# Third-stage scores from one 32-row product a batch, and the first stage without its fixed schedule of slots

## The chip, the cores and the metric

The kernel runs on one core of a Trainium2 chip. The time is the device time of one execution in microseconds, the median of three runs. The core has five engines that run side by side, each through its own list of instructions: TensorE (PE, with its weight loads as PEld), VectorE (DVE), ScalarE (ACT), GpSimd (POOL) and SyncE (SP), which here issues most DMAs. They wait for each other through semaphores.

## The reference, cut to what matters

The input x holds 128 batches of 128 tokens with 128 features, adj the edges of each batch. Four graph layers follow each other, each on a normalised and rectified copy of x and each added to x. Layer 0 averages neighbours by relation. Layer 1 builds weights from the differences of all pairs of tokens:

```
D = |x[:, :, None, :] - x[:, None, :, :]|
h = einsum('bijc,oc->bijo', D, W1) + b1       # 64 features a pair
m, v = mean and variance of h over all b, i, j
h = leaky((h - m) / sqrt(v + EPS) * g1 + be1)
s = where(A > 0, einsum('bijo,uo->biju', h, W2) + b2, NEG)
A = softmax(s, axis=-1)
```

The mean and variance run over all batches, so nothing of the second half of layer 1 can begin before all pairs have been multiplied. Layers 2 and 3 are attention layers with additive scores:

```
e_i = einsum('bnhd,d->bnh', h, a_i)           # one number a token and head
e_j = einsum('bnhd,d->bnh', h, a_j)
e = e_i[:, :, None, :] + e_j[:, None, :, :]
e = where(e > 0, e, 0.2 * e), then where(adj > 0, e, NEG)
attn = softmax(e, axis=2)
out = einsum('bijh,bjhd->bihd', attn, h)
```

Layer 2 has four heads of 32 features, layer 3 one head of 128.

## The kernel before, in words

The batches go in 32 groups of four (G = 4). The program has three stages.

**First stage: layer 0, and the pairs of layer 1.** Layer 0 of a group is a chain: load x, adj and agg; statistics and normalised copy hn; the mask of relation 1, its degree; transposes hT and maskT; products hw and po; normalisation with gamma and beta; the new x, its statistics and the normalised h1. Then h1 is transposed into xp (PSUM) and copied to xe (SBUF), with 64 columns repeated behind it, so that the feature column of token i + k is a shifted read. A batch has four tiles of pairs (NT = 4), each of 2 x 8 shifts. A tile takes four steps: the difference d = xe shifted - x (L399; tiles 0 and 2 on DVE, which reads x from xp, tiles 1 and 3 on POOL, which reads it from xe); its absolute value on ACT (L440); four products with W1 on PE into one of two hp buffers (L407); the evacuation hp to hs on ACT (L416), followed by the statistics of hs on DVE (L425, L426). Four tiles of hs fill one buffer of three, which SP stores to DRAM. d has two buffers for DVE and two for POOL.

All of this is written out by hand: slot(i) lists, for one tile number i, the difference of tile i + 2 (DVE) or i + 3 (POOL), the absolute value of tile i + 1, the products of tile i, the evacuation of tile i - 1 and the statistics of tile i - 2. features(g, half) puts the transposes and copies of two batches into given slots, with two buffers of xp, one for each half, and lets POOL copy the 64 repeated columns (L465). chain(g) puts each step of layer 0 into a slot from 22 slots ahead of the group; there hn is made on POOL (L508) and the last shift lnnb of h1 on POOL too (L195). manual_schedule keeps this order on every engine.

**Second stage: the rest of layer 1.** hs comes back from DRAM as z; the scores, the softmax and the output of layer 1 are formed. Its code is not touched.

**Third stage: layers 2 and 3.** group(g) is a generator; _staggered starts a new one every six steps, so that about five groups are under way. Here a scheduler places the instructions; so it also does for the code of the first stage that is not under manual_schedule. For each batch of layer 2, the scores e_i + e_j for four heads are summed in one PSUM tile pe by seven products: hT against A_i2, a weight column spread over 128 columns (L969), four products of A_j2 against hT (L971), a constant from the bias b_2 in three bf16 rows (L973), and the mask no_edge x off, which puts a large negative number where there is no edge (L974). Layer 3 does it with one product of 512 columns, four of 128 and the mask for the whole group (L1006, L1008, L1010). Then ACT copies pe to e (L900), DVE takes the maximum (L901) and the leaky rescale (L902), ACT the exponentials (L910), PE transposes e, ACT copies it to eT (L152), and PE multiplies with the values into pv (L989, L1021), which DVE divides by the sums (L991, L992, L1023). The normalisations take the root on POOL (L121, L122) between DVE's statistics (L127, L129) and its scaling h (L134).

Of the kernel before, what the change touches and what calls it, by code (L numbers as in the profile page):

```python
# [17 lines left out]
P = 128  # L18
G = 4
# [48 lines left out]
def tile_gnn_stack(ctx: ExitStack, tc: tile.TileContext, a: dict, out: bass.AP):  # L68
# [88 lines left out]

    with tc.tile_pool(name="c0", bufs=1) as c0, tc.tile_pool(name="p0", bufs=2) as p0:
# [12 lines left out]

        XP = [psum.tile([P, 3, P], F32, tag=f"xp{n}", name=f"xp{n}") for n in range(2)]
        gamma, beta = (t[:, 2, :] for t in XP)

# [33 lines left out]
        def layer0(g):  # L208
# [5 lines left out]
            agg = p0.tile([P, G, P], F32, name="agg")  # L214
            yield
# [35 lines left out]
            nc.vector.tensor_copy(o, po)  # L251
            yield "rest"
            nc.sync.dma_start(agg, AGG[g])
            nc.vector.tensor_tensor(o, o, agg, OP.add)
# [5 lines left out]
            for k in range(G):  # L260
                nc.vector.scalar_tensor_tensor(o[:, k, :], o[:, k, :], mv[:, k, 0:1], gamma,
                                               op0=OP.subtract, op1=OP.mult)
            yield
            on = sm("on")
            for k in range(G):
                nc.vector.scalar_tensor_tensor(on[:, k, :], o[:, k, :], rs[:, k:k + 1], beta,
                                               op0=OP.mult, op1=OP.add)
# [6 lines left out]
            H1[g] = p0.tile([P, G, P], F32, name="h1", bufs=3)  # L274
            act_norm(H1[g], x, RS1[:, g], nb)

# [5 lines left out]
        with tc.tile_pool(name="sc", bufs=1) as sc:  # L282
            top = highest(sc)
            flag = const.tile([1, 1], I32, name="flag")
            for t, v in ((gamma, "gamma"), (beta, "beta")):
                nc.vector.tensor_copy(t, load(v, [P, P], _bcast(a[v], P), pool=c0))
# [84 lines left out]

        jobs = {}

        def at(slot, engine, work):
            jobs.setdefault((slot, engine), []).append(work)  # L380

        def now(slot, engine):
            for work in jobs.pop((slot, engine), ()):
                work()

        XE, diffs, linear, halves, stats = {}, {}, {}, {}, {}

        def difference(i):

            b, t = divmod(i, NT)  # L390
            xe, k = XE[b // 2], b % 2
            on_pool = t in ON_POOL
            d = p0.tile([P, 2, KC, P], F32, tag=f"d{int(on_pool)}", name="d")
            x = xe[:, k, 0:P] if on_pool else XP[b // 2 % 2][:, k, :]
            ahead = xe[:, k, 1 + KC * t:]
            ahead = bass.AP(tensor=ahead.tensor, offset=ahead.offset,
                            ap=[list(ahead.ap[0]), [KH, 2], [1, KC], [1, P]])
            eng = nc.gpsimd if on_pool else nc.vector
            eng.tensor_tensor(d, ahead, x[:, None, None, :].to_broadcast([P, 2, KC, P]), OP.subtract)  # L399
            diffs[i] = d.rearrange("p h k i -> p h (k i)")  # L400

        def products(i):
            d = diffs.pop(i)
            hp = linear[i] = big("hp").rearrange("p a b -> p (a b)")
            for c in range(0, KC * P, 512):
                for hh in range(2):
                    nc.tensor.matmul(hp[64 * hh:64 * hh + 64, c:c + 512], w1T, d[:, hh, c:c + 512],  # L407
                                     start=True, stop=True)

        def evacuate(i):  # L410

            b, t = divmod(i, NT)
            if t == 0:
                halves[b] = p0.tile([P, NT, KC * P], F32, name="hs", bufs=3)
                stats[b] = small.tile([P, 9, 6], F32, name="st")
            nc.scalar.copy(halves[b][:, t, :], linear.pop(i))  # L416
            if t == NT - 1:
                nc.sync.dma_start(HP[b], halves[b])

        def statistics(i):  # L420

            b, t = divmod(i, NT)
            last = t == NT - 1
            hs, st = halves[b][:, t, :], stats[b]
            nc.vector.bn_stats(st[:, 2 * t, :], hs[:, 0:512])  # L425
            nc.vector.bn_stats(st[:, 2 * t + 1, :], hs[:, 512:1024 - P * last])  # L426
            if last:
                nc.vector.bn_stats(st[:, 8, :], hs[:, 1024 - P:])
                nc.vector.bn_aggr(ST1[:, b, 0, :], st.rearrange("p a b -> p (a b)"))
                nc.vector.bn_aggr(ST1[:, b, 1, :], st[:, 8, :])  # L430
                del halves[b], stats[b]

        def slot(i):
            n = NT * NB
            if 0 <= i + 2 < n and (i + 2) % NT not in ON_POOL:
                difference(i + 2)
            if 0 <= i + 3 < n and (i + 3) % NT in ON_POOL:
                difference(i + 3)
            if 0 <= i + 1 < n:
                nc.scalar.activation(diffs[i + 1], diffs[i + 1], AF.Abs)  # L440
            if 0 <= i < n:
                products(i)
            if 0 <= i - 1 < n:
                evacuate(i - 1)
            if 0 <= i - 2 < n:
                statistics(i - 2)
# [20 lines left out]
        def chain(g):  # L467
# [23 lines left out]
            def roots(last=False):  # L491
                rs = t["rs"] = RS1[:, g] if last else small.tile([P, G], F32, name="lnrs")
                rsqrt(rs, t["mv"][:, :, 1])
                if last:
                    t["nb"] = shift(t["mv"], rs)
# [570 lines left out]
```

## Time and profile before

| | |
|---|---|
| median of three runs | 3580.16 us (3574.61 to 3580.36) |
| the profiled execution's own time | 3580.16 us |
| its span | 3578.4 us |
| first stage, first to last absolute value | 89 to 1764 us |
| second stage, first to last score product | 1787 to 2757 us |
| third stage, first to last load's scaling and last output | 2809 to 3574 us |
| PE, DVE, ACT, POOL busy | 77%, 75%, 72%, 45% of the span |

Busy time is a union over the instructions of an engine. The duration of one instruction is longer than the distance to the next one's start where the two overlap; the distance between starts is what one costs in a dense row. A wait is put down to the instruction that ended it.

### The profile page before, as it was taken

To read this page: it belongs to the slowest core of one execution; us is meant where nothing else is said; L and a number is where in the kernel's file an instruction comes from. 1 tells how busy PE (TensorE), PEld (TensorE's weight loads), DVE (VectorE), ACT (ScalarE), POOL (GpSimd) and SP (SyncE) were. 2 spreads that over 40 slices of the span, in tenths; PEclk is the share of its full clock that TensorE was granted. 3 is DMA by queue.
4 is the path that set the end of the run, shared out by engine and by line. 5 is a ranking of instruction groups with operands and counts; after the bars stand their busy time and mean duration, and the time that the engine had idled before them with its cause. 6 is when DMAs were issued, how large, how long until landed. Compare 5 with 4: busy or idle time off the path is not lost.

```text
span 3578.4 us, 43595 instructions
## 1 busy us (share of the span) xinstructions
PE 2752.0 (77%) x15153; PEld 1351.2 (38%) x15153; DVE 2699.6 (75%) x5623; ACT 2593.5 (72%) x2987; POOL 1610.6 (45%) x1061
## 2 busy tenths in 40 slices
PE   1777776777777777777568888888887699999998
PEld 1222222222222222222123333333333577777776
DVE  4889888888888988988836666666666567777775
ACT  1988898898988989889756666666665366666664
POOL 2888888888889889888500000000000122222221
PEclk8989999999999999999879999999999799999998
DMA  6444444444444444444597888888885201111000
GB/s 220 162 176 183 171 177 188 182 173 174 188 176 168 185 188 176 179 174 176 205 365 266 326 325 326 325 326 326 326 326 193 79 30 36 36 34 33 22 25 18
DMA packets 168626, 659.10 MB, mean 184 GB/s; under 512 B 31312, under 2 KB 83408, under 8 KB 118224
## 3 DMA queue, kind: packets, MB, share of 16 engines
q1 hardware_dynamic: 165264, 643.65, 47.3%
q0 software_dynamic: 2560, 8.39, 0.8%
q10 hardware_dynamic: 576, 4.19, 0.3%
q8 instruction: 123, 2.02, 0.2%
q14 instruction: 103, 0.84, 0.1%
HBM read 340.76 MB, written 315.42 MB: 183 GB/s over the span
## 4 chain that ended last, share of the span: by engine, by line
PE 32%; DVE 26%; POOL 16%; ACT 11%; issue 10%; DMA 3%; SPq 0%; POOLq 0%; ACTq 0%; DVEq 0%
POOL d L399 10%; PE ps L691 8%; ACT d L440 5%; DVE z L696 4%; PE pt L151 3%; PE pk L713 3%; PE pv L989 3%; DVE d L399 3%; ACT hs L416 3%; DMA z<-hp 3%; PE hp L407 2%; DVE st L425 2%; DVE st L426 2%; PE pr L928 2%; ACT e L910 2%
## 5 line engine op out<-in xcount | busy, mean ns | idle before, releaser
L407 PE MATMUL hp<-d,w1T 128*64 128x512 f32 x4096 | 1059.6, 640 | 426.0 <-ACT hs L416 298.4
L399 POOL TENSOR_TENSOR d<-xe 128x2048 f32<-128x2048 f32 x256 | 1074.6, 4198 | 51.0 <-PE hp L407 48.4
L440 ACT ACTIVATE d<-d 128x2048 f32<-128x2048 f32 x512 | 988.8, 1931 | 57.9 <-POOL d L399 55.2
L407 PEld LDWEIGHTS hp<-d,w1T 128*64 128x64 f32 x4096 | 281.6, 142 | 1102.7 <-issue 721.8
L399 DVE TENSOR_TENSOR d<-xe,xp 128x2048 f32<-128x2048 f32 x256 | 580.1, 2266 | 11.3 <-POOL xe L465 7.7
L416 ACT COPY hs<-hp 128x1024 f32<-128x1024 f32 x512 | 523.1, 1022 | 1.2 <-PE hp L407 1.2
L425 DVE BATCH_NORM_STATS2 st<-hs 128x6 f32<-128x512 f32 x512 | 351.5, 687 | 197.5 <-ACT hs L416 196.2
L121 POOL TENSOR_SCALAR scale<-mv 128x1 f32<-128x1 f32 x1 | 0.2, 222 | 1020.7 <-DVE mv L827 1020.7
L691 PE MATMUL ps<-z,w2z 128*32 128x512 f32 x1024 | 225.1, 711 | 178.3 <-DVE z L696 164.8
L426 DVE BATCH_NORM_STATS2 st<-hs 128x6 f32<-128x512 f32 (+1 forms) x512 | 329.2, 643 | 0.0
L696 DVE SCALAR_TENSOR_TENSOR z<-z 128x2048 f32<-128x2048 f32 x128 | 291.7, 2279 | 2.5 <-ACT z L695 2.5
L700 ACT ACTIVATE zr<-z,bias,scale 128x2048 f32<-128x2048 f32 x128 | 266.7, 2084 | 30.8 <-issue 15.0
L900 ACT COPY e<-pe 128x512 f32<-128x512 f32 x160 | 93.7, 586 | 264.3 <-PE pe L974 262.3
L695 ACT ACTIVATE z<-z,bias,scale 128x2048 f32<-128x2048 f32 x128 | 266.6, 2082 | 15.9 <-DMA z<-hp 15.5
L121 POOL TENSOR_SCALAR lnrs<-lnmv 128x4 f32<-128x4 f32 x128 | 30.9, 241 | 546.2 <-DVE lnmv L129 484.8
L691 PE MATMUL ps<-z,w2l 128*32 128x512 f32 x1024 | 268.7, 688 | 0.0
L691 PE MATMUL ps<-zr,w2r 128*32 128x512 f32 x1024 | 241.1, 631 | 0.6 <-ACT zr L700 0.6
L910 ACT ACTIVATE e<-e,mx 128x128 f32<-128x128 f32 x640 | 209.3, 390 | 14.2 <-DVE mx L907 12.5
L713 PEld LDWEIGHTS pk<-pick,su 128*128 128x128 f32 x1024 | 124.3, 192 | 114.8 <-ACT y L783 24.1
L151 PE MATMUL pt<-ident,e 128*128 128x128 f32 x768 | 128.1, 294 | 40.2 <-DVE e L763 29.9
L971 PEld LDWEIGHTS pe<-hT,spread 128*128 128x128 f32 x1024 | 133.4, 193 | 47.0 <-issue 47.0
L713 PE MATMUL pk<-pick,su 128*128 128x16 f32 x1024 | 136.2, 265 | 6.8 <-DVE su L707 6.5
(226 smaller groups left out, 4468.2 us busy)
## 6 DMA issues: line engine op xcount, KB each, us to landing
hp<-hs SPq DMA_DIRECT2D x128, 2048.0 KB, 6.3
z<-hp SPq DMA_DIRECT2D x256, 1024.0 KB, 13.1
x<-x SPq DMA_DIRECT2D x128, 256.0 KB, 5.8
u<-rows SPq DMA_DIRECT2D x32, 384.0 KB, 11.5
x<-in_x_dram SPq DMA_DIRECT2D x32, 256.0 KB, 7.7
adj<-in_adj_dram SPq DMA_DIRECT2D x32, 256.0 KB, 8.1
agg<-a SPq DMA_DIRECT2D x32, 256.0 KB, 7.6
z<-y SPq DMA_DIRECT2D x32, 256.0 KB, 7.2
```

What stands on the lines that cost most here:

```text
L399: eng.tensor_tensor(d, ahead, x[:, None, None, :].to_broadcast([P, 2, KC, P]), OP.subtract)
L407: nc.tensor.matmul(hp[64 * hh:64 * hh + 64, c:c + 512], w1T, d[:, hh, c:c + 512], start=True, stop=True)
L416: nc.scalar.copy(halves[b][:, t, :], linear.pop(i))
L425: nc.vector.bn_stats(st[:, 2 * t, :], hs[:, 0:512])
L426: nc.vector.bn_stats(st[:, 2 * t + 1, :], hs[:, 512:1024 - P * last])
L440: nc.scalar.activation(diffs[i + 1], diffs[i + 1], AF.Abs)
L691: nc.tensor.matmul(ps[32 * c:32 * c + 32, :], w[:, w0:w0 + 32], v[:, 512 * c:512 * c + 512], start=j0 == 0, stop=j0 > 0 and i == 1, skip_g ...
L695: nc.scalar.activation(z0, z0, AF.Identity, bias=bias1, scale=scale1[:, 0:1])
L696: nc.vector.scalar_tensor_tensor(z0, z0, 0.01, z0, op0=OP.mult, op1=OP.max)
L700: nc.scalar.activation(zr, z1, AF.Relu, bias=bias1, scale=scale1[:, 0:1])
L713: nc.tensor.matmul(pk[:, kk, 0:16], su[:, kk, :], pick.rearrange("p h j -> p (h j)"), start=True, stop=True)
L910: nc.scalar.activation(e[:, q, :], e[:, q, :], AF.Exp, bias=mx[:, t, q:q + 1], accum_out=None if sums is None else sums[:, t, q:q + 1])
```

## The change

It has two parts.

In the first stage, the slots, features and chain are gone. Layer 0 of every group is the generator layer0, which existed before for the first two groups, woven with a generator pairs(g) by _weave, three steps of layer0 for four of pairs. The scheduler orders the instructions. There is one xp for the four batches of a group in place of two for two batches each; xe has two buffers of four batches in place of three of two; ACT makes both parts of xe; hn is made on ACT; gamma and beta lie in a PSUM tile of their own.

In the third stage, e_i and e_j are computed by token: hT of each batch is the weight, and eight columns (layer 3: two) are the moving operand. DVE writes the result into a tile of tokens whose other columns are one, with 32 columns a batch, and PE transposes it: after that, each batch owns 32 rows, in which e_i stands beside ones and ones beside e_j. ACT copies the left side, DVE multiplies the right side with a constant pattern that keeps one head (layer 3: one batch) a block of columns. One fp32 product of 32 rows (layer 3: of all 128) then gives e_i + e_j for all heads, and the mask follows as before. The bias is added in the tokens. A new group starts every seven steps.

```diff
+    def pairwise(pool, xe, xp, k, t):
+        on_pool = t in ON_POOL
+        d = pool.tile([P, 2, KC, P], F32, tag=f"d{int(on_pool)}", bufs=2, name="d")
+        x = (xe if on_pool else xp)[:, k, 0:P]
...
+        eng = nc.gpsimd if on_pool else nc.vector
+        eng.tensor_tensor(d, ahead, x[:, None, None, :].to_broadcast([P, 2, KC, P]), OP.subtract)
+        d = d.rearrange("p h k i -> p h (k i)")
+        nc.scalar.activation(d, d, AF.Abs)
+        hp = big("hp").rearrange("p a b -> p (a b)")
+        for c in range(0, KC * P, 512):
+            for hh in range(2):
+                nc.tensor.matmul(hp[64 * hh:64 * hh + 64, c:c + 512], w1T, d[:, hh, c:c + 512],
+                                 start=True, stop=True)
+        return hp
+
+    def pair_stats(pool, xe, xp, k, b):
+        st = small.tile([P, 9, 6], F32, name="st")
+        hs = pool.tile([P, NT, KC * P], F32, name="hs", bufs=3)
+        for t in range(NT):
+            yield
+            hp = pairwise(pool, xe, xp, k, t)
+            nc.scalar.copy(hs[:, t, :], hp)
+            nc.vector.bn_stats(st[:, 2 * t, :], hs[:, t, 0:512])
...
-        XP = [psum.tile([P, 3, P], F32, tag=f"xp{n}", name=f"xp{n}") for n in range(2)]
-        gamma, beta = (t[:, 2, :] for t in XP)
+        affine = psum.tile([P, 2, P], F32, tag="affine", name="affine")
...
+        def pairs(g):
+            h = H1.pop(g)
+            xp = psum.tile([P, G, P], F32, tag="xp", name="xp")
+            for k in range(G):
+                nc.tensor.transpose(xp[:, k, :], h[:, k, :], ident)
+            xe = p0.tile([P, G, P + 2 * KH], F32, name="xe")
+            nc.scalar.copy(xe[:, :, 0:P], xp)
+            nc.scalar.copy(xe[:, :, P:], xp[:, :, 0:2 * KH])
+            for k in range(G):
+                yield from pair_stats(p0, xe, xp, k, g * G + k)
...
-        with tc.manual_schedule():
-            for g in range(NG):
-                for half in range(2):
-                    features(g, half)
-                if g >= AHEAD:
-                    chain(g)
-            for i in range(-5, NT * NB + 2):
-                slot(i)
+        for g in range(NG):
+            _weave(pairs(g), layer0(g + AHEAD) if g + AHEAD < NG else iter(()), 0.75)
...
+        def sides(g, hT, wa, n):
+            ps = sm("ps")
+            for k in range(G):
+                nc.tensor.matmul(ps[:, k, 0:2 * n], hT[:, k, :], wa, start=True, stop=True)
+            t = tokens[n][g % 3]
...
+            if n == 4:
+                nc.vector.tensor_tensor(to, ps_k, add_b.rearrange("p (s h) -> p s h", s=2)[:, None, :, :]
+                                        .to_broadcast([P, G, 2, n]), OP.add)
+            else:
+                nc.vector.tensor_copy(to, ps_k)
+            yield
+            pt = sm("pts", "pt")
+            for side in range(2):
+                nc.tensor.transpose(pt[:, side, :], t[:, side, :, :].rearrange("p k c -> p (k c)"), ident)
+            yield pt
...
+            got = []
+            yield from last_of(sides(g, hT, wa2, 4), got)
+            left = p2.tile([P, P], F32, name="left")
+            nc.scalar.copy(left, got[0][:, 0, :])
+            right = p2.tile([P, 4, P], F32, name="right")
+            nc.vector.tensor_tensor(right, got[0][:, 1:2, :].to_broadcast([P, 4, P]),
+                                    heads[:, :, None].to_broadcast([P, 4, P]), OP.mult)
...
-                    nc.tensor.matmul(pe, hT[:, k, :], A_i2, start=True, stop=False, skip_group_check=True)
-                    for hd in range(4):
-                        nc.tensor.matmul(pe[:, hd, :], A_j2[:, hd, :], hT[:, k, :], start=False,
-                                         stop=False, skip_group_check=True)
-                    nc.tensor.matmul(pe, ones3, b_parts, start=False, stop=False, skip_group_check=True)
+                    rows = slice(32 * k, 32 * k + 32)
+                    nc.tensor.matmul(pe, left[rows, :], right[rows, :, :], start=True, stop=False,
+                                     skip_group_check=True)
...
-            nc.tensor.matmul(pe, A_j3[:, 0, :], hT, start=True, stop=False, skip_group_check=True)
-            for k in range(G):
-                nc.tensor.matmul(pe[:, k, :], hT[:, k, :], A_i3[:, 0, :], start=False, stop=False,
-                                 skip_group_check=True)
+            nc.tensor.matmul(pe, left, right, start=True, stop=False, skip_group_check=True)
...
-        _staggered((group(g) for g in range(NG)), 6)
+        _staggered((group(g) for g in range(NG)), 7)
```

## The prediction

> **What bounds the kernel now.** I read the busy time by stage first, then the waits of the engine that is fullest in each stage the change touches, then the timeline of one period. The span is 3578.4 us; the profiled execution's own time is 3580.16 us, which is also the median shown, so 1.8 us lie around the span and no correction is needed.
>
> By stage (busy us and instructions of each engine, granted clock, DMA):
>
> ```profile
> core 0: us, PE busy (x) PEld busy (x) DVE busy (x) ACT busy (x) POOL busy (x), PEclk, DMA share, GB/s
> 200.00:1400.00 1200.00, 870.32 (x3720) 302.64 (x3720) 1051.56 (x1993) 1073.63 (x929) 1025.34 (x587) 0.94 0.45 178
> 1770.00:2800.00 1030.00, 800.33 (x5064) 342.45 (x5064) 658.67 (x1088) 607.67 (x417) 1.56 (x4) 0.88 0.82 305
> 2892.00:3486.00 594.00, 576.58 (x3937) 465.50 (x3937) 423.82 (x1346) 370.01 (x1009) 129.63 (x181) 1.00 0.11 32
> ```
>
> First stage: ACT 89%, DVE 88%, POOL 85%: three nearly full engines. Third stage: PE 97%, DVE 71%, ACT 62%. The second stage's instruction order is the same in both programs on every engine, so I leave it alone.
>
> Who keeps ACT idle in those 1200 us (total, times, longest), and what lies there on POOL and ACT:
>
> ```profile
> ACT h L555 <- POOL lnnb L195: 67.3, 23, 3.1
> ACT d L440 <- POOL d L399: 39.6, 45, 1.5
> ACT xe L461 <- PE xp L457: 14.0, 14, 1.7
> ACT maskT L521 <- PE pt L518: 5.3, 12, 0.5
> ```
>
> ```profile
> 1020.07 0.23 POOL L121 TENSOR_SCALAR RS<-MV 128x4 f32<-128x4 f32 x1 [4.94 <-DVE MV L489]
> 1021.79 0.25 POOL L195 TENSOR_SCALAR lnnb<-lnnb 128x4 f32<-128x4 f32 x1
> 1022.00 4.18 POOL L399 TENSOR_TENSOR d<-xe 128x2048 f32<-128x2048 f32 x1
> 1075.36 0.25 POOL L195 TENSOR_SCALAR lnnb<-lnnb 128x4 f32<-128x4 f32 x1
> ```
>
> The four waits sum to 126.2 us, all of ACT's idle time (1200 - 1073.6). L195 runs once a group of four batches; eight of its steps, from 704.15 to 1127.60, give 52.93 us a group (the two shown are one of them). So ACT works 47.4 us and waits 5.6 us a group of 16 tiles. Between starts, an absolute value L440 costs 1.81 us, an evacuation L416 0.89.
>
> Third stage, PE, one batch, and the same instruction one group later; then the waits there:
>
> ```profile
> 3200.31 1.02 PE L969 MATMUL pe<-spread,hT 128*128 128x512 f32 x2
> 3201.17 1.05 PE L971 MATMUL pe<-hT,spread 128*128 128x128 f32 x8
> 3202.15 0.38 PE L973 MATMUL pe<-b_parts,ones 3*128 3x512 bf16 x1
> 3202.47 0.39 PE L974 MATMUL pe<-off,no_edge 128*128 128x512 bf16 x1
> 3202.70 1.02 PE L969 MATMUL pe<-spread,hT 128*128 128x512 f32 x2
> 3223.09 1.02 PE L969 MATMUL pe<-spread,hT 128*128 128x512 f32 x2
> ```
>
> ```profile
> DVE sums L991 <- PE pv L989: 97.1, 52, 7.8
> DVE h L134 <- POOL lnrs L122: 45.1, 52, 0.9
> PE pv L1021 <- ACT eT L152: 17.4, 26, 0.7
> ```
>
> A batch of scores costs 2.39 us between starts (0.86 + 0.98 + 0.32 + 0.23), a group 22.78 us, of which PE idles about 0.7. DVE waits for PE in long pieces; its wait for POOL's root is 0.86 us, twice a group.
>
> [...] DVE stands 0.86 us before an h at 3202.67, waiting for POOL's root, though the rescale L902 queued behind it has had its maximum since 3201.82 (L901 from 3201.13, 0.69 long). So the built order of each engine, which carries no times, decides with the durations here. [...] No 32-row product is in this trace; in the second stage, eight records of L713 between 32-column products take 0.99 us, against 0.86 for eight of the sixteen of L989 (1.71)[...].
>
> **First stage, worked out.** Added on ACT: the normalisation hn moves there from POOL, 4 x 0.395 = 1.58 us (a pair of h takes 0.79). xe is copied once a group in two pieces (0.50 + 0.27) for two copies of 0.30: +0.17. ACT's work becomes 47.4 + 1.75 = 49.1 us. POOL loses hn (3.15) and two copies (0.29 each), gains a shift (0.45): it is not the bound. DVE gains a small maximum.
>
> The waits follow from the new order at each group's start. ACT runs: xe in two pieces, evacuation 15 of the old group, abs of tile 1 (POOL's), abs of tile 0, the four h, abs of tile 3 (POOL's), abs of tile 2, evacuation 0. There is one xp buffer, so xe can't be made before tile 14's difference is done. Clock from the end of xe:
> - Evacuation 15 needs its product: 0.45 to 1.34.
> - POOL's difference of tile 1 takes 4.2: abs 1 at 4.3 to 6.1, abs 0 to 7.9. ACT idles 3.0.
> - POOL runs tile 3's difference next (to 8.6), then root 1.12 and shift 0.54: lnnb at 10.3. The four h wait until then: 2.4 idle; they end at 11.9.
> - abs 3 to 13.7, abs 2 to 15.5, evacuation 0 to 16.4; then ACT is dense but for 0.3 before evacuation 4, whose product queues behind four transposes.
> - Tile 14's difference ends at 47.8 on DVE, xp's transposes and product 14 at 52.7, evacuation 14 at 54.1, the next xe at 55.
>
> 49.1 + 0.45 + 3.0 + 2.4 + 0.3 = 55.2; the walk gives 55.0. I take 55.1, 2.2 us over 52.93. For 30 groups 66 us; the last two, without layer 0 beside them, pay the same start, some 3 us each: **+72 us**. The head (h at 82 us, behind the DMA of agg) keeps its releaser. If the new dense stretch has slack I overlooked, the period falls to about 54.4 (+50); if tile 14's difference slips past product 13, which has 0.4 us of slack, about 56 (+95).
>
> **Third stage, worked out.** Removed on PE a group: 4 x 2.39 for layer 2, and 0.86 + 0.90 + 0.22 for layer 3 (L1006, L1008, L1010): 11.5 us. Added: 4 x (0.90 + 0.23); two side products of four 128-row weights with 8 and 2 columns, by L989's 0.107 a record 8 x 0.107 = 0.86 each; four transposes 0.44; layer 3's 1.1: 7.8. PE's work falls from about 22 to 18.2 us. DVE gains two 128x512 products from PSUM (0.60 each, by L1023) and two small writes (0.14, by L717): from 423.8/594 x 22.78 = 16.3 to 17.7. ACT gains two copies of 128x128, about 0.2 each.
>
> No engine is full then, so I followed the order around one period. It has two halves in series. DVE half, from the reciprocal that waits for pv of one group to the h whose transposes PE needs next: reciprocal, max, o, rescale, three statistics, aggregates, right, small: 3.2; wait for POOL's root 0.87; h and small 1.1; two maxima and two rescales 2.4; statistics, aggregates 1.07; reciprocal, two maxima, small 1.5; two rescales 1.2; h 1.03: 12.4 us. PE stands in the transposes of h meanwhile. PE half, from there to the pv that the reciprocal awaits: hand-over and last transpose 0.17; e 0.44; pv 0.86; sides 0.86; pr 0.95; e and sides 1.3; po 0.93; sides' transposes 0.22; pv 0.86; e 0.44; wait 0.56 for layer 3's right, which DVE can make only after po and that pv; scores 1.13; pv 1.71; tail 0.13: 10.6. Sum 22.9 against 22.78: PE's 3.7 us turn into waits for DVE. 31 steps of 0.15 are +5 us, and the longer path at fill and drain +3: **+8 us**.
>
> Unknown costs. The 32-row products [...] stand where PE waits anyway, beside the DVE half; I take nothing. A side product could cost its weight loads' own 0.19 a record, +0.7 each: +45 us in all; or less than a 33-column one, 0.3 each, -19. right could cost 0.1 more: +6. Set-up: six fills on POOL behind the weights' DMA, against a spread of 1.68 us and the three-part split that go: between -3 and +3; I take nothing.
>
> Forecast: 3580.16 + 72 + 8 = **3660 us**.
>
> **Rivals.**
> - Third stage bound by its busiest engine (ends faster): if the two halves overlap and PE stays as full as now, the period is 18.2/0.97 = 18.8 us, 31 x 4.0 = -123: 3580 + 72 - 123 = 3529. It decides below 20.5 us, where 72/31 us a group pay for the first stage. For it: PE's 97% now. Against: DVE's 17.7 plus two root waits of 0.86 already make 19.4, and its reciprocal sits behind pv.
> - First stage unchanged: POOL, with 41 us of work in 53, gets ahead and the new waits vanish: 3588. Against: POOL can't start before xe exists.
> - Both worse: a missed product makes the first stage 57 us a group (+123 to +125), side products cost their loads: 3580 + 125 + 50 = 3755. For it: slack of 0.4 us.
> - The scores' part does nothing because PE was not the bound: excluded by 97%; it does what it says, and DVE is late next.
>
> **How the numbers follow.** My forecast 0.72, third stage faster 0.09, first stage unchanged 0.06, both worse 0.13. Its own bounds, +50 to +95 and -15 to +55, not all at one end, give 3605 to 3720; for the rivals I widen to 3598 to 3728. A measurement of this kernel tells about 0.2% from no change. Faster than that: 0.09; within it: 0.03, half of the first-stage rival; slower: 0.88.
>
> **What would show it.** First stage: about 55 us a group; ACT's longest waits before abs of POOL's tile and before h, at group starts. Third stage: still about 23 us a group, PE near 80%, PE waiting for DVE's h, DVE waiting for PE's pv and po. I am wrong if the third stage's period is under 21, or the first stage's is 53.

## The result, and the profile after

The changed kernel takes 3825.35 us (3821.53 to 3828.12, four runs), the kernel before beside it 3577.68 us: a ratio of 1.0692, with a 95% interval of 1.0673 to 1.071. It is 247.7 us slower; the prediction was 80 us slower, and its range ended at 3728 us.

From the trace, the first product of the second stage starts at 1945.6 us instead of 1787.0: +158.6 us for the first stage. The second stage has its old length. The rest, some 88 us, is the third stage.

The table by stage of the changed kernel (columns as in the prediction's first table: busy us and instructions of each engine, granted clock, DMA):

```profile
core 0: us, PE busy (x) PEld busy (x) DVE busy (x) ACT busy (x) POOL busy (x), PEclk, DMA share, GB/s
200.00:1400.00 1200.00, 850.21 (x3412) 276.11 (x3408) 986.80 (x1846) 1029.94 (x941) 875.44 (x440) 0.86 0.40 164
1930.00:2960.00 1030.00, 800.96 (x5064) 342.71 (x5064) 658.38 (x1091) 607.21 (x416) 2.02 (x6) 0.88 0.81 305
3073.00:3720.00 647.00, 626.90 (x3310) 434.30 (x3309) 462.15 (x1452) 395.93 (x1066) 130.57 (x182) 0.80 0.10 29
```

The column to look at is the one after POOL. The granted clock of TensorE (the share of its full rate that it was given) fell from 0.94 to 0.86 in the first stage and from 1.00 to 0.80 in the third; the untouched second stage keeps 0.88. In the third stage PE is again busy 97% of the time, although the change took work from it: the same products last longer (1.12 us becomes 2.07 for one of four in the timeline below).

The first stage in the timeline, PE's products L175 (start, us, and in brackets the idle time before and who ended it). Eight records are one tile, sixteen are two:

```profile
1015.93 1.94 PE L175 MATMUL hp<-d,w1T 128*64 128x512 f32 x8 [0.77 <-ACT d L171]
1025.59 6.38 PE L175 MATMUL hp<-d,w1T 128*64 128x512 f32 x16 [7.72 <-ACT d L171]
1033.98 5.35 PE L175 MATMUL hp<-d,w1T 128*64 128x512 f32 x16 [2.01 <-ACT hs L187]
1039.85 1.94 PE L175 MATMUL hp<-d,w1T 128*64 128x512 f32 x8
1044.70 3.63 PE L175 MATMUL hp<-d,w1T 128*64 128x512 f32 x8 [2.33 <-ACT d L171]
```

A tile takes 1.94 us, but after PE has stood still for 7.7 us at a group's start, two take 6.38; two more take 5.35 behind a wait of 2.0, and one takes 3.63 behind a wait of 2.3. The clock is 0.5 for 10.2 us from 1020.9, and for 3.4 us each from 1034.5 and 1044.8: 17 us of a 58-us group. The kernel before has such places too, but fewer: 6.1 us of a 53-us group on average (138 us of half clock between 200 and 1400 us). One of them:

```profile
1025.70 5.37 PE L407 MATMUL hp<-d,w1T 128*64 128x512 f32 x16 [2.37 <-ACT hs L416]
1032.56 1.94 PE L407 MATMUL hp<-d,w1T 128*64 128x512 f32 x8 [1.49 <-ACT hs L416]
```

What ScalarE waits for in the 1200 us of the table's first row (total, times, longest):

```profile
ACT d L171 <- POOL d L169: 60.9, 21, 2.9
ACT hs L187 <- PE hp L175: 58.4, 89, 1.4
ACT h L239 <- POOL lnnb L233: 47.1, 21, 2.2
```

The first and third rows are the waits that the prediction placed at a group's start (2.9 and 2.25 us, where 3.0 and 2.4 were expected). The middle row was not in its sum: 58.4 us in 21 groups, 2.8 us a group.

The third stage, PE's score products of one group:

```profile
3402.39 1.12 PE L848 MATMUL pe<-right,left 32*128 32x512 f32 x2
3403.44 0.39 PE L850 MATMUL pe<-off,no_edge 128*128 128x512 bf16 x1
3403.76 1.12 PE L848 MATMUL pe<-right,left 32*128 32x512 f32 x2
3404.81 0.39 PE L850 MATMUL pe<-off,no_edge 128*128 128x512 bf16 x1
3405.43 1.12 PE L848 MATMUL pe<-right,left 32*128 32x512 f32 x2 [0.23 <-DVE right L839]
3406.48 0.39 PE L850 MATMUL pe<-off,no_edge 128*128 128x512 bf16 x1
3406.80 2.07 PE L848 MATMUL pe<-right,left 32*128 32x512 f32 x2
```

The fourth takes nearly double the others, without a gap before it to speak of (0.23 us in the five before). The clock stays at 0.5 from 3407 to 3414. Outputs leave 23.3 to 26.5 us apart, 24.92 us on average over the first 27 groups, against 22.8 for most groups before. The stage's filling, before its first output, ran at a clock of 0.60, where the kernel before had 0.80, and took some 22 us more than before.

### The profile page after: what moved, and what is told of

It reads as the page before. It is cut to its first block, busy times and chain, and to the rows that moved or that the text cites. A ratio compares the mean times of both kernels' runs of the same rounds, so it can differ in the third digit from the quotient of the medians.

```text
span 3825.5 us, 42248 instructions
## 1 busy us (share of the span) xinstructions
PE 2917.1 (76%) x14385; PEld 1329.6 (35%) x14385; DVE 2767.7 (72%) x5773; ACT 2682.0 (70%) x3171; POOL 1508.8 (39%) x913
## 4 chain that ended last, share of the span: by engine, by line
PE 41%; ACT 21%; DVE 18%; issue 8%; POOL 6%; DMA 4%; SPq 0%; POOLq 0%; DVEq 0%; ACTq 0%
ACT d L171 11%; PE hp L175 8%; PE ps L531 7%; ACT hs L187 7%; PE pe L848 5%; PE pt L151 4%; POOL d L169 4%; DVE z L536 4%; DMA z<-hp 3%; PE pv L865 3%; PE pk L553 3%; DVE d L169 2%; DVE st L188 2%; DVE st L190 2%; PE pr L798 1%
## 5 line engine op out<-in xcount | busy, mean ns | idle before, releaser
L175 PE MATMUL hp<-d,w1T 128*64 128x512 f32 x4096 | 1147.5, 694 | 502.8 <-ACT d L171 437.6
L175 PEld LDWEIGHTS hp<-d,w1T 128*64 128x64 f32 x4096 | 291.5, 155 | 1189.8 <-ACT d L171 636.3
L848 PE MATMUL pe<-right,left 32*128 32x512 f32 x256 | 213.7, 926 | 2.4 <-DVE right L839 2.4
L151 PE MATMUL pt<-ident,e 128*128 128x128 f32 x768 | 157.9, 330 | 46.9 <-DVE e L603 29.8
L151 PEld LDWEIGHTS pt<-ident,e 128*128 128x128 f32 x768 | 113.8, 175 | 112.6 <-issue 84.5
```

Of the source, the lines that this page charges most:

```text
L151: nc.tensor.transpose(pt[:, k, :], src[:, k, :], ident)
L848: nc.tensor.matmul(pe, left[rows, :], right[rows, :, :], start=True, stop=False, skip_group_check=True)
```

## Experiments

Two questions. Are the half-clock stretches a cause of the time, or do they only mark waits that would be there anyway? And what brings them on: gaps on PE, or the new kinds of product? Differences in the table are against the kernel before, run beside each. An edit can shift the order in which the scheduler puts the instructions; where two kernels are compared, the text says whether they share it.

| run | what it is | us | against before |
|---|---|---|---|
| e1_third | third-stage change alone | 3671.67 | +98.2 |
| e2_first | first-stage change alone | 3731.31 | +157.8 |
| e4_fill4, e5_fill6, e6_fill12 | whole change, 4, 6, 12 fillers a group | 3817.74, 3815.75, 3820.21 | +244.3, +242.4, +246.9 |
| e8_fill_both | 12 + 8 fillers | 3751.59 | +178.2 |
| e3_rows128 | e1, masked product of 128 rows | 3677.28 | +103.8 |
| e7_all128 | e1, products of 128 rows | 3650.89 | +77.5 |
| e9_wide32 | e1, token products 64 wide | 3623.07 | +49.7 |
| e10_wide128 | both | 3611.04 | +37.7 |
| e14_gap6 | e1, six steps | 3874.72 | +301.1 |
| e16_wide6_rows32 | e14, 64 wide | 3775.09 | +198.0 |
| e11_gap6 | e10, six steps | 3555.96 | -17.4 |
| e12_masked6, e13_wide6, e15_masked5 | six or five steps, split by batch kept | 3590.06, 3604.13, 3681.25 | +16.4, +30.5, +107.6 |
| e17_pool6, e18_diag | the same | 3658.31, 3626.17 | +81.2, +52.4 |

### The two halves apart

The first run has the first stage of before and the third stage of the change; the second is the reverse.

> The change to the third stage alone; the first stage keeps its fixed schedule of slots. If the two halves of the change add up as the trace of the changed kernel divides them, this gives the kernel before plus about 88 us, near 3666 us, with a period of about 24.1 us a group in the third stage. If half of that loss was carried in from the first stage (a clock that is granted less because of what ran earlier), less than 40 us is left.

> The change to the first stage alone; the third stage keeps its old scores. If the halves add up, the kernel before plus about 159 us, near 3737 us, with a period of about 58 us a group. If the first stage's loss depends on what the third stage prepares (tables, pools), it differs from 159 by more than 20 us.

Measured: +98.2 us (ratio 1.0267, 1.0241 to 1.0293) and +157.8 us (1.0444, 1.0424 to 1.0464), together 256 against 248 for the whole. The halves add up, each has its own loss, and the third stage's is there with a first stage that runs as before: its clock is 0.80 from 2950 to 3550 us in the first of the two runs, 0.98 in the second. So the two are studied apart.

### First stage: fill PE's gaps

Filler products give PE more to do and nothing else. If they make the kernel faster all the same, the clock is the likely reason.

```diff
-        affine = psum.tile([P, 2, P], F32, tag="affine", name="affine")
+        affine = psum.tile([P, 4, P], F32, tag="affine", name="affine")
...
+            for n in range(4):
+                nc.tensor.matmul(affine[:, 2:4, :], ident, xe[:, 0:2, 0:P], start=True, stop=True)
```

> The changed kernel with four filler products (128x256, fp32[...]) a group in the first stage, issued right after the copy of xe, in TensorE's longest gap of 7.7 us; the order of ScalarE, VectorE and GpSimd is not changed. Theory A (that gap lowers the clock of the products after it, which ScalarE then waits for): the gap is cut to about 5.5 us, the two products after it take under 5 us in place of 6.4, and the first stage's period falls from 58.0 by 1 to 3 us, so 30 to 85 us off the kernel although TensorE does more. Theory B (ScalarE's waits come from the order alone): no change within 10 us.

> The changed kernel with six filler products (128x256, fp32) a group after the copy of xe in the first stage; one exponent of the order of ScalarE shifts by a tile against the changed kernel, so this run is only the partner of the one with twelve, whose instructions stand in the same order on every engine apart from the fillers. Six fillers take about 2.9 us, so about 5 us of TensorE's longest gap is left. Both theories: near 3815 us.

> The same order with twelve fillers, about 5.9 us, so that under 2 us of the longest gap is left. Theory A (the gap lowers the clock of the products behind it and ScalarE waits for these): the clock there stays at 1.0, the first two tiles behind the gap take about 4 us in place of 6, and the kernel is 30 to 80 us faster than with six fillers. Theory B (the waits come from the order alone): the same time within 10 us, or slower.

Four fillers shortened the gap only to 5.8 us; the clock fell all the same, and the time, +244.3 us, is the changed kernel's +247.7 within what the runs scatter. Six and twelve fillers, in one order, gave 3815.75 and 3820.21 us: theory B seems to win. The twelve did what they should at their place:

```profile
1019.86 5.45 PE L329 MATMUL affine<-xe,ident 128*128 128x256 f32 x24
1027.67 3.65 PE L175 MATMUL hp<-d,w1T 128*64 128x512 f32 x16 [2.37 <-ACT d L171]
1036.99 8.38 PE L175 MATMUL hp<-d,w1T 128*64 128x512 f32 x24 [5.66 <-ACT d L171]
```

The two tiles behind the filled gap took 3.65 us in place of 6.38. But a second gap, 5.66 us, follows, and the three tiles behind it took 8.38 us, where 3 x 1.94 would be 5.8. The loss had moved: ScalarE's waits of this kind were 72.3 us in 21 groups, not fewer. The period stayed at 58.0 us for most groups of all three runs, which also fits a cycle that has nothing to do with the clock. So the second gap was filled too, with eight more behind the second tile of each group, and no other engine's order changed in the steady groups:

```diff
+        for n in range(8 if (k, t) == (0, 1) else 0):
+            nc.tensor.matmul(fills[0], ident, xe[:, 0:2, 0:P], start=True, stop=True)
         return hp
```

> As the run with twelve fillers a group, and eight more after the second tile of each group, in the second long gap of TensorE (5.7 us); ScalarE, VectorE and GpSimd keep that run's order in the steady groups. Theory A (half-clock products behind gaps cause ScalarE's waits): no half-clock stretch is left in the first stage, ScalarE no longer waits 1.6 and 1.2 us for products, the period falls from 58.0 to about 55 us and the kernel is 60 to 90 us faster than with twelve fillers. Theory B (another cycle holds the period at 58.0 us): the period stays at 58.0 us whatever the clock.

Measured: 3751.59 us, 68.6 us less than with twelve fillers, although PE does eight products a group more. The table of its first stage:

```profile
200.00:1400.00 1200.00, 992.43 (x4420) 435.72 (x4422) 1047.74 (x1925) 1064.41 (x976) 907.14 (x456) 0.97 0.42 171
```

The clock is 0.97 (one stretch of 3.4 us a group is left), ScalarE's waits of 1.6 and 1.2 us for products are gone, and xe is copied every 55.0 us, with 56.7 in one group of four or five; the prediction took 55.1. The second stage begins at 1875.7 us, 88.7 us later than before. So theory A holds: of the first stage's 158.6 us, some 70 are half-clock products, and the rest goes with the new order of instructions (at a clock a little above the 0.94 of the kernel before). It takes both gaps to see it: with twelve fillers one low stretch of 6.8 us a group was left, and the period was still 58.0.

### Third stage: rows and columns

First the score product over 128 rows. Two ways: a mask made by GpSimd, and no mask at all, which adds no instruction.

```diff
+            left4 = p2.tile([P, G, P], F32, name="left4")
+            nc.gpsimd.tensor_tensor(left4, left[:, None, :].to_broadcast([P, G, P]),
+                                    batches[:, :, None].to_broadcast([P, G, P]), OP.mult)
...
-                    nc.tensor.matmul(pe, left[rows, :], right[rows, :, :], start=True, stop=False,
+                    nc.tensor.matmul(pe, left4[:, k, :], right, start=True, stop=False,
```

The second run writes left in that product in place of left4[:, k, :], and makes no left4.

> As the third-stage change alone, but the scores of the second attention are one product of all 128 rows a batch: the left factor is multiplied by a mask of the batch's 32 rows on GpSimd, so the other rows add zeros. TensorE has the same number of products of the same 128x512 output and the same waits. Theory A (products on 32 of 128 rows count as little work for the clock, so TensorE is slowed while it is busy): the clock in the steady third stage goes from 0.80 to over 0.95, the period from 24.1 to about 22.9 us, and the kernel is 30 to 80 us faster than the third-stage change alone. Theory B (the clock falls because TensorE waits for other engines): the waits are as before, so clock and time stay within 10 us of the third-stage change alone, or get a little worse by the GpSimd step.

> The third-stage change alone, with every batch's score product over all 128 rows of left and right, so that it adds the terms of all four batches (the split by batch is left out); no instruction is added, and the order of all engines is that of the third-stage change alone. Theory A (products on 32 of 128 rows count as little work for the clock): TensorE's clock in the steady third stage goes from 0.80 to over 0.95 and the period from 24.1 to about 23 us, so 25 to 60 us faster than the third-stage change alone. Theory B (TensorE's waits lower the clock): clock and time unchanged within 10 us.

In the first of the two, the mask used keeps two of a batch's 32 rows, so only two of its eight terms are in the sum; the work is the same. It was no faster (3677.28 us, with 3665 to 3697 in its four executions; the profile is of the longest): its clock over the whole execution was 0.890 where e1_third had 0.875, but the new GpSimd step (the same instruction takes 1.04 us in e17_pool6) and the handing over stand ahead of the products, and outputs came 23 to 31 us apart. That run measures the added wait as much as the rows.

The second keeps the order of every engine. It was 20.8 us faster than the third-stage change alone: less than the 25 to 60 us of theory A, and more than theory B's 10. Its clock rose from 0.80 to 0.90 (between 2950 and 3250 us), where theory A expected over 0.95. Its score products, PE alone:

```profile
3023.30 1.02 PE L1007 MATMUL pe<-right,left 128*128 128x512 f32 x2
3024.16 0.38 PE L1009 MATMUL pe<-off,no_edge 128*128 128x512 bf16 x1
3024.37 1.02 PE L1007 MATMUL pe<-right,left 128*128 128x512 f32 x2
3025.23 0.38 PE L1009 MATMUL pe<-off,no_edge 128*128 128x512 bf16 x1
3026.43 1.12 PE L1007 MATMUL pe<-right,left 128*128 128x512 f32 x2 [0.82 <-DVE right L999]
3027.39 0.38 PE L1009 MATMUL pe<-off,no_edge 128*128 128x512 bf16 x1
3027.61 1.02 PE L1007 MATMUL pe<-right,left 128*128 128x512 f32 x2
```

All four at full clock, although the gap before the third is 0.82 us where the changed kernel had 0.23. So the fall at this place does not come from that gap; it came with the 32-row products (or with their turns with products of 128 rows: the two were not told apart). Also, a batch takes 1.07 us between starts here, and 1.37 with 32 rows at full clock. Groups without a low stretch took 22.9 to 23.0 us, the prediction's 22.9. But there were few of them. The gain is all in the filling: the first output left 27 us earlier than in e1_third, and from there to the last one a group took 24.6 us on average against 24.3. Low stretches had come up at other places. The one at 2960.5 us follows 3.4 us in which PE had two waits, of 0.25 and 0.50 us; that would be theory B's cause, if in pieces. Others have no gap before them. One begins at 3015.0, behind these:

```profile
3011.62 0.31 PE L1024 MATMUL pv<-wr,eT 128*128 128x33 f32 x2
3011.76 1.03 PE L903 MATMUL ps<-wa,hT 128*128 128x2 f32 x8
3012.66 0.84 PE L1024 MATMUL pv<-wr,eT 128*128 128x33 f32 x6
3013.33 1.14 PE L958 MATMUL pr<-w,hT 128*128 128x128 f32 x8
3014.30 0.27 PE L151 MATMUL pt<-ident,e 128*128 128x128 f32 x1
3014.41 1.06 PE L903 MATMUL ps<-wa,hT 128*128 128x8 f32 x8
```

PE is recorded busy without a break, but mostly with products of 2, 8 and 33 columns. Neither theory had that. Theory C, a guess from this trace alone: narrow products lower the clock as well. The token products of e_i and e_j are new in the change; widening them is nearly free (eight records take 1.03 and 1.06 us here with 2 and 8 columns, and 1.00 us with 64 in e11_gap6).

```diff
-            wa = c2.tile([P, 2 * n], F32, name=f"wa{n}")
-            nc.vector.tensor_copy(wa, pv[:, 0, 0:2 * n])
+            wa = c2.tile([P, 64 // (2 * n), 2 * n], F32, name=f"wa{n}")
+            nc.vector.tensor_copy(wa, pv[:, 0:1, 0:2 * n].to_broadcast([P, 64 // (2 * n), 2 * n]))
...
-                nc.tensor.matmul(ps[:, k, 0:2 * n], hT[:, k, :], wa, start=True, stop=True)
+                nc.tensor.matmul(ps[:, k, 0:64], hT[:, k, :], wa, start=True, stop=True)
```

> The third-stage change alone, with the token products of e_i and e_j 64 columns wide in place of 8 and 2: the weight vectors are repeated, and the extra columns are not read. The products last about as long[...]. Theory C (the clock follows how densely the array is used, so narrow products and 32-row products both lower it): the half-clock stretches that begin behind the narrow products go, those that begin in the 32-row products stay; clock 0.80 to about 0.85, 10 to 30 us faster than the third-stage change alone. Theory B (only waits matter): no change within 10 us.

> The run with 128-row score products (split by batch left out), with the token products 64 columns wide. Theory C: hardly a half-clock stretch is left in the steady third stage, clock over 0.95, period 23.0 us in nearly every group, and 30 to 55 us faster than with 128-row products alone, within 35 us of the kernel before. Theory B: the stretches stay where TensorE waits, no change within 10 us.

Measured: 48.6 us faster than the third-stage change alone with 32 rows (expected 10 to 30), and 39.9 us faster with 128 rows. The order of ScalarE and GpSimd is unchanged, VectorE's but for a few instructions of the filling. In the first, a stretch of 6.8 us or more stays in most groups, and it begins in or just behind the 32-row products; most groups took 23.2 to 23.6 us. In the second the clock is 0.95 and about half of the groups took 22.8 or 22.9 us, where nearly every one was expected to; of the stretches that are left, those at 3072.4 and 3099.7 us follow the two short waits. So in these runs the clock rose with the width of the token products (from 0.80 to 0.83 between e1_third and e9_wide32) and with the rows of the score products (from 0.83 to 0.95 between e9_wide32 and e10_wide128). For short waits close together this run alone does not show it: most groups have the same two waits and no fall (see the last section).

### Six steps between groups

The change also goes from six steps to seven. With PE at full clock, what does that do?

> The run before with a new group every six steps, as in the kernel before, in place of seven. If the two serial halves (VectorE, then TensorE) come from the seven steps, the period falls below 22 us; if they come from the chain inside a group, it stays at about 23 us or gets longer.

Measured: 3555.96 us, 55 us faster than with seven steps and 17.4 us faster than the kernel before (0.9939, 0.9921 to 0.9958), with most outputs 21.0 us apart. The two serial halves of 22.9 us belong to the seven steps. It does not split the scores by batch, so this is a measurement of the order and not a better kernel. Now the same six steps with the change's own products, and with only the width mended. These three share the order of ScalarE, VectorE and GpSimd but for a few instructions in the filling:

> The third-stage change alone with six steps between groups, as in the kernel before, and nothing else changed. If the seven steps cost what they cost with 128-row products (55 us), about 3615 us; if the half-clock stretches take the gain back, within 15 us of the third-stage change alone.

> The six-step run of the third-stage change alone with token products 64 columns wide; the score products keep 32 rows, and the order of ScalarE, VectorE and GpSimd is that of the six-step runs with narrow products (3875 us) and with 128 rows and 64 columns (3556 us). If the narrow products are what keeps TensorE at half clock there, this run falls to 3570 to 3610 us; if the 32-row products are, it stays above 3750 us.

Measured: 3874.72, 3775.09 and 3555.96 us (the second with one execution of four at 3730.84). The first is slower than anything else here; neither of its expectations allowed it. One period of it, and one of the run with 128 rows and 64 columns:

```profile
3166.00:3200.00 34.00, 31.96 (x126) 22.36 (x127) 17.64 (x57) 15.26 (x41) 5.13 (x7) 0.60 0.07 24
```

```profile
3103.00:3124.00 21.00, 19.59 (x128) 14.82 (x128) 17.20 (x57) 14.79 (x42) 5.12 (x7) 1.00 0.13 39
```

VectorE and ScalarE do the same 17 and 15 us of work in both. PE is busy 94% of one and 93% of the other, with about as many records; apart from the products' rows and columns only the clock differs, and the period goes from 21 to 34 us. The low stretch lasts 27.3 us of each 34.1 us: at full clock it would have been half as long, an estimate, and 34.1 - 13.65 = 20.5. So the clock accounts for nearly all of it. Of the 319 us between the ends, the width is 100 and the rows are 219. The longer time of the 32-row products themselves, 1.37 against 1.07 us a batch, can make at most 4 x 0.30 x 32 = 38 of the 219. With seven steps PE is busy 89% of the time at a clock of 0.95 (e10_wide128) and 97% at 0.80 (e1_third): slow products fill its waits, and the same two edits are worth 61 us; with six steps PE is busy 93% (e11_gap6, clock 0.96), and the others wait for it (ScalarE's e for 152 of 600 us).

### Versions that compute the reference

Four ways to split left by batch with six steps. ScalarE makes four scaled copies (with five steps too), GpSimd multiplies by a mask, or VectorE writes each batch into a tile of its own that is zero elsewhere and PE transposes four tiles; and the 32 rows of the change. The token products of e12_masked6, e13_wide6 and e15_masked5 were 128 columns wide, filled with zeros, and not 64 as the first expectation has it, and their order is another one, which differs among the three too.

```diff
-            nc.scalar.copy(left, got[0][:, 0, :])
+            for k in range(G):
+                nc.scalar.activation(left[:, k, :], got[0][:, 0, :], AF.Copy, scale=own_rows[:, k:k + 1])
```

> The kernel before with the third-stage change alone, six steps between groups, token products 64 columns wide, and score products over 128 rows with the split by batch restored: ScalarE makes four masked copies of the left factor (scale by a column that is one on the batch's rows) in place of one copy. If ScalarE's three extra copies (about 0.8 us a group, by the 0.27 us of the copy of left) stay in its idle time, the period is near 21 us and the time near 3555 to 3570 us, under the kernel before. If they stand on the chain, up to 25 us more, and no gain is left.

> As that, but with the 32-row score products of the change. If 32-row products lower the clock wherever they stand, each group has a half-clock stretch of 3.5 to 7 us and the time is 20 to 60 us above the masked version. If it was the waits of the seven-step order that made them costly, the two are within 10 us.

> The masked version with five steps between groups. If fewer groups' steps between two starts keep TensorE and VectorE busier, below the six-step version; if buffers (five of most tiles, six of x) hold the next group back, the same or slower by 10 us and more.

> The six-step run with 128 rows and 64 columns, with the split by batch restored by one GpSimd product a group (mask times left); ScalarE and VectorE keep their order. The GpSimd step adds about 1.3 us between the copy of left and the first score product. If that delay is covered by other groups' work on TensorE, 3556 to 3572 us, which computes the reference and is below the kernel before; if it stands on the chain, up to 35 us more than 3556.

> The kernel before with the third-stage change, six steps, 64-column token products and 128-row score products, which compute the reference in another way: VectorE writes e_i of each batch into a tile of its own that is zero outside the batch's columns, and TensorE transposes four such tiles, so that left is split by batch with no mask. Added a group: three transposes (0.3 us), a wider copy on ScalarE (0.3 us), one small VectorE write (0.2 us), and no GpSimd step. If these stand beside other work, 3556 to 3575 us, under the kernel before or level with it; if they shift the order into a chain with waits of 3 us on TensorE, as in the run with masked copies on ScalarE, 3585 to 3620 us.

None beats the kernel before. The nearest, 3590.06 us (1.0045, 1.0032 to 1.0059), goes in threes of 20.5, 21.5 and 26.2 us: the long one has a PE wait of 2.9 us for eT, and the clock falls there for 6.8 us. With 32 rows it is 14 us slower, less than expected: low stretches of 3.4 us come once in two groups; that the token products of 128 columns keep the clock up there is likely, and not shown. Five steps are worse by 91 us; why was not followed up. e18_diag has a clock of 0.97 and 23.7 us in most groups: there the order is what is left to cost, with VectorE waiting 2.7 us a group for the transposes of the tokens. Both e17_pool6 and e18_diag are slower than either of their expectations allowed. In e17_pool6, which has the order of e11_gap6 on ScalarE and VectorE, PE's wait before the tokens' transposes grows from 0.47 to 1.22 us. First e11_gap6, then e17_pool6:

```profile
3113.39 0.41 PE L917 MATMUL pts<-ident,tokens 128*128 128x128 f32 x2 [0.47 <-DVE sums L1026]
3114.93 1.87 PE L1024 MATMUL pv<-wr,eT 128*128 128x33 f32 x16
```

```profile
3153.23 1.03 PE L1029 MATMUL pv<-wr,eT 128*128 128x33 f32 x8
3155.48 0.41 PE L919 MATMUL pts<-ident,tokens 128*128 128x128 f32 x2 [1.22 <-DVE sums L1031]
3156.15 1.16 PE L1012 MATMUL pe<-right,left 128*128 128x512 f32 x2 [0.26 <-DVE right L1004]
3157.11 3.46 PE L1029 MATMUL pv<-wr,eT 128*128 128x33 f32 x16
```

Behind it eight products of 33 columns (sixteen records) take 3.46 us in place of 1.87, the clock stays low for 6.8 to 10.2 us, and most groups take 25 to 27 us in place of 21. Three quarters of a microsecond of waiting cost some five. So in this run the fall came with a wait of 1.22 us.

## Why the prediction was wrong

**First stage, +72 us.** The walk through the order was right: the two waits at a group's start are there at 2.9 and 2.25 us, and without nearly all low stretches the period is 55.0 us against the 55.1 taken. Measured that way the stage costs 88.7 us, inside the bounds of 50 to 95. Part of the 17 us above the forecast lies at the head, which the prediction took as unchanged: the first copy of xe starts at 96.3 us, in the kernel before at 85.9. The step that failed is "then ACT is dense but for 0.3 before evacuation 4": ScalarE waited 2.8 us a group for products. The products' durations were those of before, at before's clock. By the same walk PE has nothing to multiply from 0.45 to 7.9 us after xe, for the first abs that its next product needs ends there (7.7 us measured); what that does to the next products was not asked.

**Third stage, +8 us.** The serial halves of 22.9 us were right as well: groups at full clock take 22.8 to 23.0 us. The steps that failed are that the 32-row products "stand where PE waits anyway, beside the DVE half; I take nothing" and the side products priced by their duration alone. Their own time is a small term (a batch takes 1.37 us where 1.13 was taken, 1 us a group; the side products take 0.90 where 0.86 was taken), but with them the clock of the whole stage was 0.80, against 0.95 with 128 rows and 64 columns. From the first output to the last the stage took 748.2 us against 682.5 before, +65.7 where 5 were taken for the periods, and the filling some 22 us more where 3 were taken for filling and drain together; in the filling too the clock was low (0.60, and 0.74 with 128 rows and 64 columns, where none of the 22 us is left). "No engine is full then" failed with it: at a clock of 0.80 PE is busy 97% of the time.

**The rivals.** The one that ends faster, a period near PE's share, needed another stagger as well as a full clock: it shows at 21.0 us in e11_gap6, and the sum's 18.8 us was too low. The slower one had the right sign and named the wrong mechanism. (In the range, the forecast's own bounds of +50 and -15 give 3615 us at the least, not 3605.) A rival with the clock was missing, though the granted clock stood in the first table that was read: 0.94, 0.88 and 1.00 were printed, and treated as constants of the kernel. The trace of the kernel before could have called for one: every record of the clock in it is 0.50 or 1.00, and of its 97 low stretches 93 last 3.4, 6.8 or 10.2 us. In the changed kernel it is the same for 161 of 166; in its first stage waits of 2.0 and 2.3 us came before two of them.

## What to carry to other kernels

A TensorE duration from a profile holds at the clock granted there: a tile of the first stage took 1.94 us at 1.00 and 3.63 at 0.50. When an edit takes dense products away, opens gaps or puts narrow products in, price the rest of PE's work at half clock too, and keep that sum as a rival: here such edits came with a clock of 0.86 for 0.94 in one stage and of 0.80 for 1.00 in another. Before believing that PE "waits anyway", try fillers: dense products that nothing reads, in every gap behind which the clock falls, tell whether the clock is what the others wait for. Filling one gap of two told nothing here (3820.21 us with twelve fillers, 3815.75 with six), filling both gave 3751.59. And try unread columns on narrow products: 64 columns in place of 8 and 2 cost PE next to nothing (1.00 us for 1.03 and 1.06) and took 49 us off.

## What the runs showed of the hardware

**The clock fell while PE was recorded busy.** In e1_third and the changed kernel it fell to 0.50 behind 3.4 us in which PE was busy 93 to 100% by its records, in or behind products of 32 rows, or of 2, 8 and 33 columns. With 128 rows and 64 columns in the same order (e10_wide128) the falls at these places went, and the clock was 0.95 in place of 0.80. Such products did not always bring it: the kernel before has eight products of 33 columns in a row, and one of 3 rows a batch, at a clock of 1.00. Whether the rows themselves count, or the turns of 32-row and 128-row products, was not told apart.

**Where the low stretches start.** In the traces of the kernel before and of the changed kernel, all of them (97 and 166) start a whole number of steps of 3.413 us apart; in the changed kernel for instance at 1020.87, 1034.52, 1044.76 and 1078.90 us, 4, 3 and 10 steps. In e10_wide128 the starts at 2953.0, 3072.4 and 3099.7 us are 35 and 8 such steps apart. There, PE was recorded busy 78% in the step before 3072.4 us and in the one before 3099.7, and also in those from 2976.8, 3045.1 and 3123.6 us, behind which the clock stayed at 1.00. So the recorded busy share alone does not decide. Two periods are near whole numbers of steps: 58.0 us in the first stage is 17, 34.1 us in e14_gap6 is 10. Whether that is why fillers in one gap left the period at 58.0 was not tested.

**A fall lasted though PE was busy.** With six steps and the change's own products (e14_gap6) five falls between 3160 and 3310 us come behind a step in which PE was busy 59 to 62%, and then the clock stays at 0.50 for 27.3 of each 34.1 us, while PE is recorded busy 92 to 100% in each step. What keeps it low was not shown.

**Width cost next to nothing.** Four products of a 128x128 weight took, at full clock, 1.03 us with 2 columns and 0.96 to 1.06 with 8 (e7_all128), 1.00 with 64 (e11_gap6) and 1.06 with 128 (e12_masked6).
